# Starting the second layer inside the first layer's last batch, and folding the experts' biases in beside the fifth unit

## The chip, the cores and the metric

The kernel runs on one core of a Trainium2 chip. A core has five engines with an instruction queue each: TensorE (PE, matrix products), VectorE (DVE), ScalarE (ACT), GpSimd (POOL) and SyncE (SP), which here issues most DMA transfers. An engine works through its own queue in order and waits on semaphores for the others. The metric is the device time of one execution in microseconds (us), as a median over several runs.

## The reference

Two layers on an image stack x of shape 4 batches x 32 x 128 x 128, with a residual around each.

```python
# layer 0, Fourier neural operator with attention over the 32 images of a batch
xn = inorm(xa)
k, q, v = fno_layer(xn, K...), fno_layer(xn, Q...), fno_layer(xn, V...)   # 32 heads
p_attn = softmax(einsum('bntk,bnsk->bnts', qf, kf) / sqrt(Hs * Ws))
p = fno_layer(einsum('bnts,bnsk->bntk', p_attn, vf), P...)
a = inorm(p + xa)
m = fno_layer(inorm(a), m0..., inner_norm=True, act=True)    # gelu
m = fno_layer(m, m1..., inner_norm=True)
x = x + inorm(m) + a

# layer 1, on 4 x 4096 tokens of 128 channels; attention in 16 pieces of 1024 tokens
f, g = x @ W1[:h], x @ W1[h:]
scores = einsum('bija,a->bij', tanh(f[:, :, None] + g[:, None] + b1), w2[:, 0]) + b2
e = exp(scores) * strictly_lower_triangle
t = t + (e / (e.sum(-1) + 1e-10)) @ layernorm(t)
# experts: softmax router, best 2 of 8, renormalised
t = t + sum of the two experts' (layernorm(t) @ expert_w + expert_b) by their weights
```

The excerpt is shortened: in the attention of layer 1 the scores are made from the normalised tokens too, and layer 0's own input is group normalised.

## The kernel before, in words

**Layer 0** is the function `layer0`, ordered by a tile scheduler from its data flow and program order. It goes through four batches `b`. For each there are: spectra of 32 images (matrix products with Fourier matrices); `attention_weights`, whose scores come from a loop over 17 columns of modes (L473 to L479: a product `pa` or `pb` on DVE or POOL, then four products on PE into `sp`) and end in `sc`, its maximum `mx` (L509) and the softmax; the value products, which multiply rows of spectra `xb`, fetched by SP in many loads (L702), with the constants `gb` (L717, L719) and contract them (`po`, L722); `py` (L739), the inverse transforms `four` (L257) with `q` added up (L752); a first set of spectra; Gelu (L847); a second set of spectra (`forward`: `pz` L233, `px` L242 and L243, weights L797 to L804); the last inverse transforms, whose updates (L905) give x1, stored in DRAM by SP (L910) in four stores per batch. `attention_weights` of the next batch is called inside the batch before; that of batch 0 is called ahead of the loop, after the constants `mcw`, `energy` and `cross` of the two multiplier layers (L591 to L613), which wait for `mcw_raw` to be loaded.

Pools of SBUF memory in layer 0: constants (with the large `gb`), images (two slots), groups, small, modes, a large one, and `xb` (four buffers). Two PSUM banks have the tag "wide", of which short products use one at a time.

**Layer 1** is `layer1`, called when layer 0 has returned and its pools are closed. It has 16 chunks `c` of 8 blocks of 128 tokens. To prepare a chunk is: load `xc` from x1 (SP), norm (`bn_stats`, `bn_aggr`, a power on POOL, and the scaling that gives `kx`), transposes `pt` (L1065) and their copy `xt` (L1066), products `pz` with `mk` and `mq` (L1082, L1093), an Exp on ACT each (L1083, L1094), a scaling on POOL (L1085), and copies between partitions by DMA (`kf`, `ke`, `qf`; `prepare` has them). The tanh is a rational function of these exponentials: for three groups of hidden units, PE forms a denominator `d` and a numerator `n` (L1297).

A unit is a stretch of 512 queries against a few blocks of keys. The loop over units `u` stands under a manual schedule, so it runs as it is written: `products(u)` (the `d` of unit u beside the `n` of unit u-1), Ln of `d` (L1350), n times r (L1355, DVE), two additions on POOL (L1358, L1359), Exp(-Ln) (L1362), Exp of the score (L1366), and the mask and attention product `po` of units further back (L1316). Preparation of the next chunks (`todo`) and output of finished ones (`ended`) are lists of small pieces, each with a cost on DVE and POOL and a kind that says whether it uses the spare PSUM bank "m"; after every unit some are taken from them by these costs and by the unit at which they are due.

Ahead of the loop stood the opening (L928 to L1100): identity, row of parameters, router `wr` and experts `we`, `eb` loaded; biases folded into the weights by three products `pm` with a matrix `mean` (L972 to L984), all through bank "m"; `mq` and `mk` (L997), constants `sgv`, `off`, `kmul`; chunk 0 prepared whole, chunk 1 loaded and normed (on DVE, POOL's power apart); then unit 0.

Of the kernel before, what the change touches and what calls it, by code (L numbers as in the profile page):

```python
# [7 lines left out]
F32 = mybir.dt.float32  # L8
AF = mybir.ActivationFunctionType
ALU = mybir.AluOpType  # L10
AX = mybir.AxisListType
PSUM = bass.MemoryType.PSUM

P = 128
B, T, H, C = 4, 32, 128, 128
# [5 lines left out]
A = 16  # L21
GROUP_SIZES = (6, 5, 5)
DSCALE = 128.0
NE = 8
IC = 1024
NB = IC // P
# [5 lines left out]
B1, W2, RB = 11, 27, 43  # L32
NSMALL = 51
# [41 lines left out]
NM = KX * KY  # L75
# [29 lines left out]
def layer0(  # L105
    tc, x, kq_modes, kq_mirror, vcw, pcw, m0cw, m1cw, mcol0, heads, heads_row, small_row, by_p, inv_cols, dram, x1
# [4 lines left out]
    const, ps, images = (p.__enter__() for p in pools)  # L111
# [21 lines left out]
    def columns(n):  # L133
# [25 lines left out]
    gb = const.tile([P, 2, 2, NM], F32, name="gb")  # L159
# [7 lines left out]
        tc.tile_pool(name="l0_modes", bufs=1),  # L167
    ]
    grp, small, modes = (p.__enter__() for p in work)
# [409 lines left out]


# [44 lines left out]
    prep_pool.__exit__(None, None, None)  # L625
    work = [tc.tile_pool(name="l0_big", bufs=1), tc.tile_pool(name="l0_xb", bufs=4)]
    big, late = (p.__enter__() for p in work)
    pools += work
    weights = attention_weights(0, front)

    for b in range(B):
# [63 lines left out]
        for x0 in range(0, KX, NK):  # L695
# [36 lines left out]
            nc.scalar.copy(rs[:, x0 : x0 + nk].rearrange("p x y -> p (x y)"), po)  # L732
        yf = big.tile([P, T, 2, KY], F32, name=f"yf_{b}", tag="spec")
# [126 lines left out]
        if b + 1 < B:  # L860
            normed = image_sums(b + 1, loaded)

# [53 lines left out]
def layer1(tc, x1, w1t_in, signs, vec17, expert_w, expert_b, router_w, small_row, out):  # L916
    nc = tc.nc
    nblk = T
    pools = [
        tc.tile_pool(name="l1_const", bufs=1),  # L920
        tc.tile_pool(name="l1_keys", bufs=2),
        tc.tile_pool(name="l1_work", bufs=2),
        tc.tile_pool(name="l1_small", bufs=2),
        tc.tile_pool(name="l1_ps", bufs=1, space=PSUM),
    ]
    const, keys, work, small, ps = (p.__enter__() for p in pools)

    tc.keep_in_program_order(nc.scalar.preload_act_table_set("natural_log_exp_and_others"))  # L928
    ident = const.tile([P, P], F32, name="ident1")
    make_identity(nc, ident)  # L930
    par = const.tile([P, NSMALL], F32, name="par1")
    nc.sync.dma_start(out=par, in_=small_row.partition_broadcast(P))
    nhalf = const.tile([P, 1], F32, name="nhalf1")
    nc.vector.memset(nhalf, -0.5)
    wr = const.tile([P, NE], F32, name="wr")
    nc.sync.dma_start(out=wr, in_=router_w)
    we = const.tile([P, NE, C], F32, name="we")
    nc.scalar.dma_start(out=we, in_=expert_w.rearrange("e d c -> d e c"))

    later = const.tile([P, 2, P], F32, name="later")  # L940
    nc.gpsimd.memset(later, 1.0)
    nc.gpsimd.affine_select(
        out=later,
        in_=later,
        compare_op=ALU.is_gt,
        fill=0.0,
        base=0,
        pattern=[[0, 2], [1, P]],
        channel_multiplier=-1,
    )  # L950

    rank = const.tile([P, NE], F32, name="rank")
    for e in range(NE):
        nc.vector.memset(rank[:, e : e + 1], float(NE - e))

    centre = const.tile([P, P + 1], F32, name="centre")
    nc.vector.tensor_scalar(centre[:, :P], ident, 1.0 / C, None, ALU.subtract)
    nc.vector.memset(centre[:, P:], 1.0 / C)

    banks = ["m"]  # L960

    def misc(name):
        banks.append(banks.pop(0))
        return ps.tile([P, 512], F32, name=name, tag=banks[-1])

    mean = const.tile([P, P], F32, name="mean")
    nc.vector.memset(mean, 1.0 / C)
    eb = work.tile([P, NE, C], F32, name="eb", tag="xt", bufs=1)  # L970
    nc.scalar.dma_start(
        out=eb.rearrange("p e c -> p (e c)"),  # L972
        in_=expert_b.rearrange("e c -> (e c)").partition_broadcast(P),
    )
    for w, row in (
        (wr, par[:, RB : RB + NE]),
        (we[:, :4].rearrange("p e c -> p (e c)"), eb[:, :4].rearrange("p e c -> p (e c)")),
        (we[:, 4:].rearrange("p e c -> p (e c)"), eb[:, 4:].rearrange("p e c -> p (e c)")),
    ):
        n = w.shape[1]  # L980
        pm = misc("pm")[:, :n]
        nc.tensor.matmul(pm, mean, w, start=True, stop=True)
        nc.vector.tensor_tensor(w, w, pm, ALU.subtract)
        nc.vector.scalar_tensor_tensor(w, row, 1.0 / C, w, ALU.mult, ALU.add)  # L984

    sg = const.tile([A + 1, P], F32, name="sg")
    nc.sync.dma_start(out=sg, in_=signs)
    w1t = const.tile([A, 2, P], F32, name="w1t")  # L990
    nc.sync.dma_start(out=w1t, in_=w1t_in)
    v17 = const.tile([A + 1, 2], F32, name="v17")
    nc.sync.dma_start(out=v17, in_=vec17)
    mq, mk = (const.tile([P, P], F32, name=n) for n in ("mq", "mk"))
# [6 lines left out]
    sgv = const.tile([P, 2], F32, name="sgv")  # L1001
    nc.vector.tensor_copy(sgv, pv[:, :2])

    one = const.tile([P, 1], F32, name="one1")
# [4 lines left out]
    off = const.tile([P, 2], F32, name="off")  # L1009
# [3 lines left out]
    kmul = const.tile([P, 1], F32, name="kmul")  # L1013
# [10 lines left out]
    def norm_pieces(src, dst, nb, beside=True):  # L1024


        st = small.tile([P, NB, 6], F32, name="st", tag="ln_st", bufs=3)
        mv = small.tile([P, NB, 2], F32, name="mv", tag="ln_mv", bufs=3)
        r = small.tile([P, NB], F32, name="r", tag="ln_r", bufs=3)
        mr = small.tile([P, NB], F32, name="mr", tag="ln_mr", bufs=3)  # L1030
        engine = nc.gpsimd if beside else nc.vector

        def stats(k0):
            for k in range(k0, k0 + 2):
                nc.vector.bn_stats(st[:, k], src[:, k])

        def aggregate(k0):
            for k in range(k0, k0 + 4):
                nc.vector.bn_aggr(mv[:, k], st[:, k])

        def scale():
            v = slice(0, nb)
            engine.tensor_scalar(r[:, v], mv[:, v, 1], 1e-5, None, ALU.add)
            nc.gpsimd.tensor_tensor(r[:, v], r[:, v], nhalf.to_broadcast([P, nb]), ALU.pow)
            engine.tensor_tensor(mr[:, v], mv[:, v, 0], r[:, v], ALU.mult)
            engine.tensor_scalar(mr[:, v], mr[:, v], 1.0, None, ALU.subtract)

        def apply(k0):
            for k in range(k0, k0 + 2):
                engine.tensor_scalar(  # L1050
                    dst[:, k], src[:, k], r[:, k : k + 1], mr[:, k : k + 1], ALU.mult, ALU.subtract
                )

        sums = [(NONE, 0.6, 0.0, lambda k=k: stats(k)) for k in range(0, nb, 2)]
        after = [(NONE, 0.6, 0.0, lambda k=k: aggregate(k)) for k in range(0, nb, 4)]
        after += [gap, (NONE, 0.0, 2.3, scale), gap]
        for k in range(0, nb, 2):
            after += [(NONE, 0.0, 1.6, lambda k=k: apply(k)), gap]
        return sums, after
# [8 lines left out]
    def prepare(b, i0, own, beside):  # L1068
# [4 lines left out]
        xc = work.tile([P, NB, C], F32, name="xc", tag="xc", bufs=4)  # L1073
        nc.sync.dma_start(out=xc, in_=x1[b, i0 : i0 + NB].rearrange("t w c -> w t c"))
        own_kx = kx[:, i0 : i0 + NB]
        xt = work.tile([P, IC], F32, name="xt", tag="xt", bufs=1)
        qe, qf = (work.tile([P, IC], F32, name=n, tag=n, bufs=3) for n in ("qe", "qf"))

        def as_keys(h):
# [4 lines left out]
            ks = work.tile([P, 512], F32, name="ks", tag="ks", bufs=1)  # L1084
# [13 lines left out]
        load = [(NONE, 0.0, 0.0, lambda: None), gap] * 2  # L1098
        sums, after = norm_pieces(xc, own_kx, NB, beside)
# [4 lines left out]
        return (qe, qf), load + sums + after, pieces  # L1104
# [114 lines left out]
    chunks = [(b, i0) for b in range(B) for i0 in range(0, nblk, NB)]  # L1219
# [10 lines left out]
    state = {}  # L1230
    sums = {}
    live = {}

    def begin(c, beside=True):
        b, i0 = chunks[c]
        if i0 == 0:

            own = (keys.tile([P, nblk, C], F32, name=f"kx_{b}", tag="kx"),) + tuple(
                keys.tile([P, nblk * P], F32, name=f"{n}_{b}", tag=n) for n in ("ke", "kf")
            )  # L1240
        else:
            own = state[c - 1][0]
        qs, norm, pieces = prepare(b, i0, own, beside)
        state[c] = (own, qs)
        return norm, pieces

# [87 lines left out]
    ]  # L1334
    norm, pieces = begin(0, beside=False)
    norm_1, todo = begin(1, beside=False)
    for piece in norm + pieces + norm_1:
        piece[-1]()
# [4 lines left out]
    with tc.manual_schedule():  # L1343
        for u in range(len(units) + 4):
# [35 lines left out]

            if starts and u >= starts[0][0] and not todo:
                _, c, end = starts.pop(0)
                todo = sum(begin(c), [])
# [34 lines left out]
    for p in reversed(pools):  # L1418
        p.__exit__(None, None, None)
# [72 lines left out]
```

## Time and profile before

| | us |
|---|---|
| median of 3 runs | 3216.72 (3215.26 to 3219.33) |
| the profiled execution, its time | 3214.14 |
| its span | 3212.4 |
| PE busy | 2971.1 (92%) |
| ACT busy | 2323.7 (72%) |
| DVE busy | 2317.7 (72%) |
| POOL busy | 2134.2 (66%) |
| last matmul of layer 0 (L257) starts at | 1092.64, for 1.14 |
| first score product of unit 0 (`d`, L1297) | 1126.64 |
| Ln of unit 1 (L1350) | 1139.11 |

Times in the trace are counted from the span's start. A line of a timeline or of the chain of waits starts with its start and its duration; for a timeline, brackets at its end give how long the engine was idle before, and what it was waiting for. `x8` is the number of instructions joined in the line. The busy shares are means over both layers: layer 0 takes about the first third of the span.

### The profile page before, as it was taken

How to read it: one execution, taken by the hardware profiler on the slowest of the kernel's cores; microseconds unless marked ns; L12 is line 12 of the kernel's file. 1: busy time of each engine (PE TensorE's matmuls, PEld its weight loads, DVE VectorE, ACT ScalarE, POOL GpSimd, SP SyncE). 2: the span in 40 equal slices, each digit the busy share in tenths (PEclk: the TensorE clock that was granted, in tenths of full speed). 3: DMA queues.
4: the chain of work that ended last, by engine and by line, in shares of the span. 5: the costliest groups of instructions: out<-in, count | busy, mean ns of one | idle time of the engine just before them, and what ended most of it. 6: DMA issues, size and time to landing. Idle time of an engine off the chain costs nothing.

```text
span 3212.4 us, 53393 instructions
## 1 busy us (share of the span) xinstructions
PE 2971.1 (92%) x19698; PEld 1558.3 (49%) x19698; DVE 2317.7 (72%) x5072; ACT 2323.7 (72%) x3205; POOL 2134.2 (66%) x1879
## 2 busy tenths in 40 slices
PE   7899899899898699999999999999999999999997
PEld 5378367458558544444344443444444434444443
DVE  5767767768777556777666868866777777687887
ACT  2344344354344389999999999998999999999992
POOL 1631641461460278878788897889878889888773
PEclk7899899999998799999999999999999999999998
DMA  6301310230130111010110000011100010101000
GB/s 137 102 25 24 100 50 3 63 108 1 39 107 1 55 45 30 7 31 8 30 37 24 14 24 14 8 32 30 29 24 14 14 37 24 37 1 31 14 14 14
DMA packets 151925, 112.57 MB, mean 35 GB/s; under 512 B 36750, under 2 KB 140273, under 8 KB 151057
## 3 DMA queue, kind: packets, MB, share of 16 engines
q1 hardware_dynamic: 135825, 103.40, 12.0%
q10 hardware_dynamic: 15840, 5.77, 0.8%
q8 instruction: 156, 2.56, 0.3%
q14 instruction: 104, 0.85, 0.1%
HBM read 68.16 MB, written 20.00 MB: 27 GB/s over the span
## 4 chain that ended last, share of the span: by engine, by line
PE 59%; POOL 11%; ACT 8%; DVE 7%; issue 5%; DMA 0%; POOLq 0%; DVEq 0%; ACTq 0%; SPq 0%
PE d L1297 19%; PE po L1316 11%; PE px L1185 6%; ACT r L1350 4%; PE n L1297 4%; PE po L722 3%; POOL e L1359 3%; POOL e L1358 3%; PE four L257 2%; PE pv L252 2%; PE px L243 2%; PE px L242 2%; POOL kx L1050 1%; ACT e L1366 1%; PE pz L233 1%
## 5 line engine op out<-in xcount | busy, mean ns | idle before, releaser
L1355 DVE TENSOR_TENSOR r<-n,r 128x1024 f32<-128x1024 f32 (+1 forms) x1056 | 962.1, 953 | 479.9 <-PE n L1297 392.5
L1358 POOL TENSOR_TENSOR e<-r 128x512 f32<-128x512 f32 x528 | 673.0, 1275 | 268.7 <-DVE r L1355 268.1
L1350 ACT ACTIVATE r<-d 128x1024 f32<-128x1024 f32 (+1 forms) x1056 | 792.9, 802 | 65.5 <-PE n L1297 58.8
L1362 ACT ACTIVATE r<-r 128x1536 f32<-128x1536 f32 x528 | 783.5, 1484 | 16.7
L1359 POOL TENSOR_TENSOR e<-e,r 128x512 f32<-128x512 f32 x528 | 671.2, 1271 | 41.4
L1297 PE MATMUL d<-qe,ke 32*128 32x512 f32 (+3 forms) x2304 | 610.0, 604 | 38.3 <-ACT r L1350 36.5
L1316 PE MATMUL po<-e,kx 128*128 128x512 f32 (+3 forms) x1152 | 594.7, 605 | 15.0 <-POOL e L1371 15.0
L1297 PE MATMUL n<-qe,ke 32*128 32x512 f32 (+3 forms) x2304 | 607.4, 603 | 0.0
L1297 PE MATMUL d<-qf,kf 32*128 32x512 f32 (+3 forms) x2304 | 554.8, 556 | 0.0
L1297 PE MATMUL n<-qf,kf 32*128 32x512 f32 (+3 forms) x2304 | 554.5, 556 | 0.0
L1189 DVE SCALAR_TENSOR_TENSOR xc<-px,wgt,xc 128x128 f32<-128x128 f32 x1024 | 358.3, 350 | 41.2 <-PE px L1185 10.4
L1366 ACT ACTIVATE e<-e 128x512 f32<-128x512 f32 x528 | 325.6, 617 | 65.1 <-POOL e L1359 64.3
L1316 PEld LDWEIGHTS po<-e,kx 128*128 128x128 f32 x1152 | 175.6, 188 | 393.5 <-issue 310.1
L1297 PEld LDWEIGHTS d<-qe,ke 32*128 32x128 f32 x2304 | 177.4, 184 | 359.7 <-ACT r L1350 340.3
L717 POOL TENSOR_TENSOR u<-xb,gb 128x858 f32<-128x858 f32 (+1 forms) x120 | 234.8, 1987 | 115.1 <-PE po L722 104.7
L1297 PEld LDWEIGHTS d<-qf,kf 32*128 32x128 f32 x2304 | 221.5, 187 | 177.1 <-issue 164.7
L804 POOL TENSOR_TENSOR spec<-spec,part 128x264 f32<-128x264 f32 x64 | 55.0, 860 | 377.2 <-DVE part L801 173.6
L1185 PE MATMUL px<-we,x2t 128*128 128x512 f32 x512 | 265.2, 603 | 6.9 <-DVE xc L1189 6.0
L719 DVE TENSOR_TENSOR u<-xw,gb 128x858 f32<-128x858 f32 (+1 forms) x200 | 206.5, 1083 | 48.5 <-PE po L722 32.4
L1297 PEld LDWEIGHTS n<-qf,kf 32*128 32x128 f32 x2304 | 228.9, 186 | 19.8 <-issue 12.5
L722 PE MATMUL po<-u,pr 128*32 128x429 f32 (+1 forms) x1280 | 187.7, 537 | 18.3 <-POOL u L717 8.7
L1297 PEld LDWEIGHTS n<-qe,ke 32*128 32x128 f32 x2304 | 177.8, 183 | 10.0 <-DVE r L1355 1.2
(353 smaller groups left out, 4185.9 us busy)
## 6 DMA issues: line engine op xcount, KB each, us to landing
xb<-xd SPq DMA_DIRECT2D x128, 214.5 KB
xc<-x SPq DMA_DIRECT2D x31, 512.0 KB
x<-x SPq DMA_DIRECT2D x16, 512.0 KB
qf<-qe SPq DMA_DIRECT2D x64, 128.0 KB
out<-xc SPq DMA_DIRECT2D x15, 512.0 KB
xb<-xd SPq DMA_DIRECT2D x32, 198.0 KB
gb<-gd SPq DMA_DIRECT2D x4, 1056.0 KB
x<-in_x SPq DMA_DIRECT2D x8, 512.0 KB
```

What stands on the lines that cost most here:

```text
L717: nc.gpsimd.tensor_tensor(u, xb, gk, ALU.mult)
L722: nc.tensor.matmul(po[32 * j : 32 * j + 32], pr[:, i, k], u[:, r], start=i == 0 and k == 0, stop=i == 3 and k == 1,)
L1185: nc.tensor.matmul(px, x2t[:, k * P : (k + 1) * P], we[:, e0 : e0 + 4], start=True, stop=True)
L1189: nc.vector.scalar_tensor_tensor(xc[:, k], px[:, e], wgt[:, k, e0 + e : e0 + e + 1], xc[:, k], ALU.mult, ALU.add)
L1297: nc.tensor.matmul(o, k, q, start=turn == 0 or g > 0, stop=turn == 1 or g > 0)
L1316: nc.tensor.matmul(sums[c, h][:, q0 : q0 + c1 - c0], kx[:, jb], e[:, c0:c1], start=jb == 0, stop=is_last and q0 > 2 * P, skip_group_check= ...
L1350: nc.scalar.activation(r[:, g], d, AF.Ln, scale=1.0 / DSCALE)
L1355: nc.vector.tensor_tensor(r[:, g], part, r[:, g], ALU.mult)
L1358: nc.gpsimd.tensor_tensor(e, r[:, 1], r[:, 2], ALU.add)
L1359: nc.gpsimd.tensor_tensor(e, e, r[:, 0], ALU.add)
L1362: nc.scalar.activation(r, r, AF.Exp, scale=-1.0)
L1366: nc.scalar.activation(e, e, AF.Exp)
```

## The change

`layer1` becomes a generator with two parts. `kernel` starts it, hands its `send` to `layer0` as `first`, and lets it run on when layer 0 has ended. Layer 0 calls `first` in batch 3, after the last Gelu's table switch, in the place where the other batches do the sums of the next one's images.

- The first part makes what chunk 0 needs (`ident`, `nhalf`, three small loads, `mq`, `mk`, `sgv`, `off`, `kmul`), loads chunks 0 and 1 into `spare`, a free image slot, by two loads of 512 KB on SP, norms both, and does chunk 0's transposes, products, Exps, scalings and copies. It uses layer 0's PSUM tiles "wide", and SBUF in a new pool on the right side, which takes the place of `gb`, `modes` and `xb`: these now lie on that side and are given up in batch 3 after the value products. The scheduler puts its instructions where their operands are ready.
- The second part makes the other constants and begins with the units. Chunks whose number divides by 3 take their `qe`, `qf` from that pool, others from the work pool with two buffers in place of three.
- The three products that fold in the biases, with their DVE work, become `biases()`, called once in unit 4, ahead of that unit's pieces. `eb` shares its memory with `x2` in place of `xt`.
- In layer 0, `attention_weights(0, front)` and the pools it needs stand ahead of `mcw`, `energy`, `cross`, no longer behind them.

Order on the engines: all orders are as before but for batch 0's attention (DVE), batch 3 of layer 0, and layer 1 up to unit 5. Steady units are untouched, and the number of instructions is the same on each engine.

```diff
@@ layer0
-    const, ps, images = (p.__enter__() for p in pools)
+    right = [tc.tile_pool(name="l0_gb", bufs=1, side="right"), tc.tile_pool(name="l0_modes", bufs=1, side="right")]
+    const, ps, images, values, modes = (p.__enter__() for p in pools + right)
...
+    prep_pool.__exit__(None, None, None)
+    pools.append(tc.tile_pool(name="l0_big", bufs=1))
+    right.append(tc.tile_pool(name="l0_xb", bufs=4, side="right"))
+    big, late = (p.__enter__() for p in (pools[-1], right[-1]))
+    weights = attention_weights(0, front)
     mcw, energy, cross = [], [], []
...
-    weights = attention_weights(0, front)
...
             nc.scalar.copy(rs[:, x0 : x0 + nk].rearrange("p x y -> p (x y)"), po)
+        if b + 1 == B:
+            for p in reversed(right):
+                p.__exit__(None, None, None)
...
         if b + 1 < B:
             normed = image_sums(b + 1, loaded)
+        else:
+            first((ps, images))
@@ layer1
+    before, images = yield
+    first_pool = tc.tile_pool(name="l1_first", bufs=1, side="right")
+    first = first_pool.__enter__()
+    spare = images.tile([P, T, C], F32, name="spare", tag="x")
...
+    def misc(name):
+        if not pools:
+            return before.tile([P, 512], F32, name=name, tag="wide")
...
+    FIRST = (slice(0, NB), slice(0, NB)), (slice(3 * NB, 4 * NB), slice(NB, 2 * NB))
...
+    _, pieces = begin(0)
+    kx = state[0][0][0]
+    norms = [normed(spare[:, r], kx[:, i], 0, i.start, False) for r, i in FIRST]
+    for piece in norms[0] + pieces + norms[1]:
+        piece[-1]()
+    yield
...
-    for w, row in (
-        (wr, par[:, RB : RB + NE]),
...
+    def biases():
+        for w, row in (
+            (wr, par[:, RB : RB + NE]),
+            (we[:, :4].rearrange("p e c -> p (e c)"), eb[:, :4].rearrange("p e c -> p (e c)")),
+            (we[:, 4:].rearrange("p e c -> p (e c)"), eb[:, 4:].rearrange("p e c -> p (e c)")),
+        ):
+            n = w.shape[1]
+            pm = misc("pm")[:, :n]
+            nc.tensor.matmul(pm, mean, w, start=True, stop=True)
+            nc.vector.tensor_tensor(w, w, pm, ALU.subtract)
+            nc.vector.scalar_tensor_tensor(w, row, 1.0 / C, w, ALU.mult, ALU.add)
...
-    norm, pieces = begin(0, beside=False)
-    norm_1, todo = begin(1, beside=False)
-    for piece in norm + pieces + norm_1:
-        piece[-1]()
+    _, todo = begin(1)
...
+            if u == 4:
+                biases()
             if starts and u >= starts[0][0] and not todo:
@@ kernel
+        second = layer1(tc, x1, *weights, out)
+        next(second)
         layer0(
...
             x1,
+            second.send,
         )
-        layer1(
...
+        for _ in second:
+            pass
```

## The prediction

> **What bounds the kernel now.** I read the page first, for what is busy on the whole and where it isn't.
>
> ```profile
> PE 2971.1 (92%) x19698; PEld 1558.3 (49%) x19698; DVE 2317.7 (72%) x5072; ACT 2323.7 (72%) x3205; POOL 2134.2 (66%) x1879
> ...
> PEclk7899899999998799999999999999999999999998
> ```
>
> TensorE (PE) bounds the mean, but a mean says nothing of one place. The clock row dips near slices 14 and 15, where layer 0 ends. So next the chain of waits there: start, length, what it followed.
>
> ```profile
> 1093.81 0.35 SPq L932
> ...
> 1094.21 5.26 DMA wr<-in_router_w
> ...
> 1103.35 2.09 PE pm L982 x2
> ...
> 1114.27 2.04 DVE kx L1050 x8
> ...
> 1126.64 2.00 PE d L1297 x2
> ...
> 1130.65 3.71 PE d L1297 x6
> ```
>
> Layer 0's last matmul ends at 1093.8. Then one thing after another: a load of the router (5.26 us), biases of the experts, mq and mk, chunk 0's norm, its transposes, its products `pz`. Layer 1's first score product `d` starts at 1126.6. For 33 us no engine is the bound; latencies are. The windows (time, then busy of PE, its weight loads, DVE, ACT, POOL, then PE's clock, DMA share, GB/s) show this stretch and the first units:
>
> ```profile
> 1094.00:1095.00 1.00, 0.00 (x0) 0.00 (x0) 1.00 (x12) 0.00 (x0) 0.90 (x4) 0.62 1.02 278
> ...
> 1127.00:1139.00 12.00, 12.00 (x39) 5.17 (x39) 0.69 (x1) 4.16 (x5) 1.56 (x1) 0.52 0.29 66
> 1139.00:1142.00 3.00, 2.34 (x35) 2.10 (x36) 2.42 (x3) 2.86 (x3) 1.58 (x2) 1.00 0.00 0
> 1142.00:1152.00 10.00, 9.30 (x62) 4.08 (x58) 5.47 (x6) 9.83 (x14) 9.10 (x9) 1.00 0.22 51
> ```
>
> From 1139 on ACT is the bound (9.83 of 10). So whatever brings ACT's units forward shortens the whole run, and what delays ACT there lengthens it. I measure the boundary by the start of the second unit's Ln (L1350), at 1139.11 in the timeline of ACT.
>
> **The change, part by part** (negative: shorter).
>
> *A. Batch 0's attention goes ahead of the mode constants.* DVE's timeline:
>
> ```profile
> 82.23 0.29 DVE L591 COPY mcw<-mcw_raw 128x66 f32<-128x66 f32 x1 [2.54 <-DMA mcw_raw<-in_m1cw]
> 82.44 1.21 DVE L473 TENSOR_TENSOR pb<-xp,xm 128x1024 f32<-128x1024 f32 x1
> ...
> 85.10 1.21 DVE L473 TENSOR_TENSOR pa<-xp,xm 128x1024 f32<-128x1024 f32 x1
> ...
> 107.33 0.68 DVE L509 TENSOR_REDUCE mx<-sc 64x16 f32<-64x512 f32 x1 [5.28 <-PE sc L498]
> ```
>
> Products `pa`, `pb` on DVE feed PE at 1.13 us apiece. Before, DVE waits 2.54 us for `mcw_raw`, and small constants stretch the run: 0.21, then 2.66−1.13=1.53 between the rows at 82.44 and 85.10, then 0.38 and 0.64 in the next two distances: 2.76. Afterwards all constants stand behind the last `pa`, where DVE waits 5.28 us for `sc` anyway, which hides their 2.8 us. That is −5.3 at best. If POOL's `pb` (1.88 us each, two per three steps: 3.8 against DVE's four at 4.5) or the images' loads gate instead, it is 0. The next row is DVE's own pitch, so I take −5.2. Without the 5.28 us wait it would keep 2.5.
>
> *B. Batch 3 carries two loads and chunk 0's and 1's norms.* Two 512 KB loads into `spare` go on SP's queue at batch 3's start. They wait for the stores of x1 of batch 2 to finish; the `xb` loads of the value products stand behind them. SP's last such store is issued near 892.2, the next `xb` at 895.4, and of four `xb` buffers three are ahead, each good for some 3.4 us of value products, 10 us: taken as 0. On DVE: 16 bn_stats of 0.21, 16 aggregates of 0.07, 16 scalings of 0.26 and a few small ones, 9 us; and two POOL powers of 1.67, on a POOL that is idle for 31.67 us up to 989.38. DVE's timeline has the cover:
>
> ```profile
> 963.28 1.12 DVE L180 TENSOR_SCALAR yf<-py 128x512 f32<-128x512 f32 x1 [6.98 <-PE py L739]
> 967.30 0.28 DVE L180 TENSOR_SCALAR yf<-py 128x64 f32<-128x64 f32 x1 [2.90 <-PE py L739]
> 971.21 0.69 DVE L752 TENSOR_TENSOR q<-q,four 128x512 f32<-128x512 f32 x1 [3.63 <-PE four L257]
> ```
>
> 6.98+2.90+3.63 is 13.5 us of idle time for 9 us. The second power comes late for the first `q` add (about 0.9), and six scalings (1.5) fall into the q stage, where PE is busy 17.30 of 18 us and DVE 13.53; DVE's spare takes about 1.2 of it. So +1.2, from 0.5 to 2.5; with no cover it would be 9.
>
> *C. Chunk 0's keys and queries stand in front of layer 0's last spectra.* PE's idle of 4.63 us before 1031.59 hides the two `pm`. From there PE runs without a gap to 1044 (12.00 of 12 us), so what is added counts in full. At full clock: `pv` and `pc` 0.5; eight transposes 1.1 (four took 0.66 at 1138.86); four `pz` of 0.86, 3.45 (one took 1.13 with its end). Their Exps (0.67 each) stand behind ACT's last Gelus and this row of its timeline:
>
> ```profile
> 1043.21 1.28 ACT L121 ACT_TABLE_LOAD   x1
> ```
>
> Two banks hold `pz`, so the third waits for the first Exp, which may come only after 1044.5. `px` of the next group then follows; by my count it goes from 1046.45 to about 1051.7: +5.3, between 4 (ACT in time) and 12 (PE held until all four Exps are done). POOL's two scalings (1.6 each) lie in an idle POOL, the ten copies of `kf`, `ke`, `qf` on an idle SP, and 44 us ahead of their use.
>
> *D. The boundary.* The first `d` waits for the banks that the last L905 update frees, at 1094.94; nothing else is late (ACT's Ln stands behind the issue of the expert loads, 0.4 us each, done by 1095.5). `d` of unit 0 costs 2.00+3.71=5.7 by the chain's two rows, and from its end (1134.36) to the second Ln passed 4.75. Both ran at half clock. At that price the Ln comes at 1095.0+5.7+4.75=1105.4: −33.7. At full clock both halve, nearly (2.85 and 2.6): 1100.4, −38.7.
> Which clock? The row 1094 to 1095 shows 0.62 already, and 1095 to 1100 has 0.50; the matmuls before it are the same in both kernels. Getting it back took all 12 us of gapless PE from 1127 to 1139. The Trainium skill ("TensorE: Matmul & The Clock Gate", Part 1, "What you observe") says that the transition "happens around 4µs into sustained matmul activity". By it the clock would be whole at 1099, `d` done at 1099.9 and the Ln at 1102.5: −36.6. The trace disagrees with it here (12 us), so I take the row: −33.7. Both ends, −31.5 (the third unit cold as well) and −38.7, go into the range.
>
> *E. Biases in unit 4.* One bank serves three products. By PE's timeline unit 5's `d` starts at 1151.46. Now `pm` of the router waits for its subtraction, behind `r<-n` that ends at 1151.47; then twice 0.96 for `pm` at full clock and 0.69 for DVE's subtraction; then `pz`, 1.06. `d` starts at about 1156.0. ACT's Ln has a little slack, and moves less:
>
> ```profile
> 1150.25 1.50 ACT L1350 ACTIVATE r<-d 128x1024 f32<-128x1024 f32 x2
> ...
> 1154.26 1.50 ACT L1350 ACTIVATE r<-d 128x1024 f32<-128x1024 f32 x2
> ```
>
> from 1154.26 to about 1157.9: +3.65, between 2.5 and 4.5. ACT is full there, so it isn't won back. The loads of the experts are issued at 1095 and used 15 us later; they took under 6.3.
>
> Sum: −5.2+1.2+5.3−33.7+3.65 = −28.75. The profiled execution took 3214.14 us (span 3212.4), so 3185.4; on the median of 3216.72, 2.6 above it, 3188.
>
> **Rivals.**
> 1. *PE stalls behind ACT in layer 0's last batch* (C at 12). For: PE takes its work in order, and Gelus and a table load stand before the Exps. Against: the first `pz` come early in a 12 us stretch in which ACT works 7.18 us. −22: 3195.
> 2. *The early move gives nothing* (A at 0). For: POOL's 3.8 is close to DVE's 4.5. Against: POOL waits for DVE's `pa` there. −23.5: 3193.
> 3. *The boundary closes only by half*, so that the change doesn't do what it says: unit 0 waits for something of layer 0's end that the router's load hid, such as the last stores of x1 (issued at 1095.66). Against: the keys come from a tile of its own, and reads of x1 aren't needed. With 17 us lost of the 34: 3205.
> 4. *Slower:* the loads into `spare` hold SP's queue at batch 3's start. The stores they wait for would have to land late: the first 10 us are covered by `xb` buffers, and the net gain of 29 more, so that it is slower only from a hold of 39 us on; at 45, +6: 3223. Against: a store of 512 KB near 892 needs no such time, as loads at the boundary moved 278 GB/s (the row 1094 to 1095), by which 512 KB take 2 us.
>
> **How the numbers follow.** The likeliest, 0.62: 3188, with its own range 3180 to 3193 (down: D at full clock −5, and B, C, E at their low ends −0.7−1.3−1.15; up: D with a cold third unit +2.2, B and E high +2.1). Rival 1 0.15, rival 2 0.12, rival 3 0.08, rival 4 0.03. Range: 3177 (those low ends, and 3 for the spread of the runs around their median) to 3200 (rivals 1 and 2 together), leaving out rivals 3 and 4 and some tails. A difference under 0.2%, 6.4 us, can't be told from none. Faster 0.96, within 0.02, slower 0.02.
>
> **What would show each step.** A: no wait for `mcw_raw` inside the `pa` run, and `mx<-sc` near 102. B: first `q` add about 1 us later against the end of `py`; SP's first `xb` of batch 3 not later. C: gap between the last Gelu and `px` of the second group 5 us longer. D: `d` of unit 0 right behind the last L905, clock 0.50 under it, second Ln 10 us later. E: an idle ACT of 3 to 4 us ahead of unit 5's Ln. The prediction is wrong if the first `d` waits longer than 2 us for anything, if `xb` loads starve, or if PE shows gaps over 5 us between the Gelus and `px`.

## The result, and the profile after

The changed kernel took 3193.26 us (median of 4 runs, 3183.4 to 3196.28) beside 3215.99 for the kernel before: a ratio of 0.9923, with a 95% interval of 0.9900 to 0.9947. Measured again, beside the experiments below, it took 3195.28 beside 3219.55: 0.9917, 0.9903 to 0.9931. So it is faster by 23 to 24 us, where 28.75 were forecast; the forecast range held the time (3177 to 3200), while the likeliest case's own range (3180 to 3193) ends just below it. The profiled execution of the changed kernel took 3196.28 us, its span is 3194.2.

Lines of kernel.py have moved: `four` is L261, the last updates L914, `d` and `n` L1349, Ln L1399, `pm` L1172. These are the page's busy shares and the clock row of the changed kernel:

```profile
PE 2961.2 (93%) x19698; PEld 1556.6 (49%) x19698; DVE 2318.6 (73%) x5072; ACT 2324.8 (73%) x3205; POOL 2135.8 (67%) x1879
...
PEclk8899999899998799999999999999999999999998
```

Sums hardly move; the work is the same. The chain of waits at the boundary, changed kernel:

```profile
1098.27 5.13 PE four L261 x24
...
1103.42 1.14 DVE x L914 x4
1104.56 0.14 issue
1104.69 3.79 PE d L1349 x8
```

The first `d` starts 0.14 us after the last update. All of the router's load, folds, norms, transposes and `pz` are gone from this place. ScalarE's timeline shows the Ln that I measured by (second row), and what came later:

```profile
1108.48 1.51 ACT L1399 ACTIVATE r<-d 128x1024 f32<-128x1024 f32 x2 [8.28 <-PE d L1349]
1113.53 1.51 ACT L1399 ACTIVATE r<-d 128x1024 f32<-128x1024 f32 x2 [2.02 <-PE n L1349]
...
1124.67 1.50 ACT L1399 ACTIVATE r<-d 128x1024 f32<-128x1024 f32 x2
1135.77 1.51 ACT L1399 ACTIVATE r<-d 128x1024 f32<-128x1024 f32 x2 [2.28 <-PE n L1349]
```

Two things strike at once. Layer 0 ends at 1104.55, no longer at 1094.94, so something in it cost much more than the +1.3 of steps A to C. And between the Ln of units 4 and 5 lie 11.1 us.

To find where it went I cut each profiled execution into stretches between the same instructions. Each number is a distance in a timeline, in us: `pa`, `mx` and Ln count by their starts, the others by their ends; "changed" gives the first and the second profile of the changed kernel, "before" the profile of the prediction and a second one, `before_again`.

| stretch | before | changed | forecast of the difference |
|---|---|---|---|
| first `pa` to `mx` of batch 0 | 36.2, 44.7 | 36.3, 36.8 | −5.2 (A) |
| last `py` of batch 3 to the last Gelu | 75.9, 73.2 | 75.2, 78.3 | +1.2 (B) |
| last Gelu to last `px` | 19.05, 19.04 | 25.82, 25.81 | +5.3 (C) |
| last `px` to the last scalars `cq` | 13.69, 13.69 | 18.45, 16.79 | 0 |
| `cq` to the last update of layer 0 | 19.0, 19.1 | 20.3, 18.9 | 0 |
| last update to Ln of unit 1 | 44.2, 44.7 | 8.98, 8.98 | −33.7 (D) |
| Ln of unit 4 to Ln of unit 5 | 4.01, 4.01 | 11.10, 8.22 | +3.65 (E) |

Those stretches repeat well. Two others don't, in any kernel: the first `pa` starts near 61 or near 70 (before: 71.1 and 60.9), and from `mx` of batch 0 to the first `py` of batch 3 it takes between 851 and 862 us. So a comparison of just two profiles is off by up to 10 us before batch 0 is done, and the ends of two spans say less than the table. From the Ln of unit 20 to the end of the span every profile takes 2002.4 to 2005.9 us, the three with the old layer 1 as well as the others: two buffers in place of three for `qe` and `qf` cost nothing that shows.

### The profile page after: what moved, and what is told of

Read it like the earlier page. It is cut to its first block, busy times and chain, and to the rows that moved or that the text cites. A ratio compares the mean times of both kernels' runs of the same rounds, so it can differ in the third digit from the quotient of the medians.

```text
span 3194.2 us, 53401 instructions
## 1 busy us (share of the span) xinstructions
PE 2961.2 (93%) x19698; PEld 1556.6 (49%) x19698; DVE 2318.6 (73%) x5072; ACT 2324.8 (73%) x3205; POOL 2135.8 (67%) x1879
## 4 chain that ended last, share of the span: by engine, by line
PE 56%; POOL 12%; ACT 9%; DVE 7%; issue 6%; DMA 0%; POOLq 0%; DVEq 0%; ACTq 0%; SPq 0%
PE d L1349 18%; PE po L1368 10%; PE px L1255 6%; ACT r L1399 4%; PE n L1349 3%; POOL e L1408 3%; POOL e L1407 3%; PE po L726 3%; PE four L261 2%; PE pv L256 2%; PE px L247 2%; PE px L246 2%; ACT e L1415 2%; POOL kx L1014 2%; DVE r L1404 2%
## 5 line engine op out<-in xcount | busy, mean ns | idle before, releaser
L1399 ACT ACTIVATE r<-d 128x1024 f32<-128x1024 f32 (+1 forms) x1056 | 793.4, 803 | 71.5 <-PE n L1349 57.8
L1349 PE MATMUL d<-qe,ke 32*128 32x512 f32 (+3 forms) x2304 | 606.7, 603 | 39.7 <-ACT r L1399 36.4
L1349 PE MATMUL n<-qe,ke 32*128 32x512 f32 (+3 forms) x2304 | 606.2, 601 | 0.0
L1349 PE MATMUL n<-qf,kf 32*128 32x512 f32 (+3 forms) x2304 | 552.3, 554 | 0.0
L1349 PE MATMUL d<-qf,kf 32*128 32x512 f32 (+3 forms) x2304 | 550.8, 554 | 0.0
L1349 PEld LDWEIGHTS d<-qe,ke 32*128 32x128 f32 x2304 | 176.9, 184 | 359.5 <-ACT r L1399 340.1
L1349 PEld LDWEIGHTS d<-qf,kf 32*128 32x128 f32 x2304 | 220.5, 186 | 176.9 <-issue 164.2
L1349 PEld LDWEIGHTS n<-qf,kf 32*128 32x128 f32 x2304 | 228.0, 185 | 18.6 <-issue 11.2
L1349 PEld LDWEIGHTS n<-qe,ke 32*128 32x128 f32 x2304 | 177.8, 183 | 9.3 <-DVE r L1404 0.9
```

Of the source, the lines that this page charges most:

```text
L1349: nc.tensor.matmul(o, k, q, start=turn == 0 or g > 0, stop=turn == 1 or g > 0)
L1399: nc.scalar.activation(r[:, g], d, AF.Ln, scale=1.0 / DSCALE)
```

## The experiments

Each but before_again, which ran once, was timed in the same rounds as runs of the kernel before; each was profiled. Ratios are to the kernel before.

**after_again** is the changed kernel, unedited.

> The changed kernel as it is, as the measure for the runs beside it. The first measurement gave 3193.3 against 3216.0, 22.7 less. If the shortfall against the forecast (28.75 less) is of the kernel and not of that one chip, the gain is 20 to 25 again; if it was an accident of the clock's phase, it comes out at 27 to 31.

Measured: 0.9917 (0.9903 to 0.9931), 24 us less. The shortfall against 28.75 repeats: it is of the kernel.

**before_again** is the kernel before, profiled once more.

> The kernel before, profiled a second time, to see which of its stages repeat. If the first stage's length is a matter of the clock's phase and not of the change, the first pa comes near 61 or near 71 here as it does in the changed kernel. If the clock's fall between the last px of layer 0 and cq is the change's doing, that stretch takes 13.7 us again, as in the first profile; if it is chance, 16 to 19 as in the changed kernels.

Measured: 3216.44 us. The first `pa` came at 60.9, so the early start isn't the change's doing. The stretch after the last `px` was 13.69 again; so the longer one is. The early start also showed that DVE's wait for `mcw_raw` ends at nearly the same time, at 81.25 here and 82.23 in the first profile. DVE's timeline of this run:

```profile
81.25 0.20 DVE L591 COPY mcw<-mcw_raw 128x66 f32<-128x66 f32 x1 [11.82 <-DMA mcw_raw<-in_m1cw]
```

It waited 11.82 us, not 2.54: the earlier `pa` starts, the longer the wait that step A takes away.

**a_undone** and **a_only**: step A taken out of the changed kernel, and put alone into the kernel before.

```diff
 # a_undone, against the changed kernel
-    weights = attention_weights(0, front)
     mcw, energy, cross = [], [], []
...
     nc.vector.tensor_mul(pv, pv, psw2)
+    weights = attention_weights(0, front)
```

> The changed kernel with batch 0's attention weights back behind the mode constants, nothing else moved. The prediction's step A expects it 5.2 us slower than the changed kernel. What the trace after suggests (ScalarE copies xw from xb before spt, waits until the loads of xb land at 89.7, and TensorE's clock halves while it waits for spt, so that the gain in the pa run is lost before mx) expects no difference: within 2 us.

> The kernel before with step A alone: batch 0's attention weights ahead of the mode constants. The prediction's step A expects 5.2 us less than the kernel before, and mx 5 to 8 us earlier for the same start of pa (from the first pa to mx 36 in place of 44.7 with an early start, 31 in place of 36.2 with a late one). If later stages take it back, because their half clocks fall differently, mx is earlier and the time within 2 us of the kernel before.

Measured: a_undone 3200.58 (0.9928, 0.9911 to 0.9946), 5 us above after_again by the medians, with overlapping intervals. a_only 3212.48 beside 3221.30: 0.9972 (0.9961 to 0.9982), 9 us less, 6 to 13 by the interval. From `pa` to `mx` a_undone took 44.5 us with its early start, as before_again. a_only took 30.8 with a late one, where the kernel before took 36.2: 5.4 less. So step A is real and was worth at least what was forecast. My suspicion that it gives nothing came from setting one early start beside one late start, and it fell. What had fed it is there, though. ScalarE's timeline of the changed kernel (early start):

```profile
89.73 0.52 ACT L715 COPY xw<-xb 128x429 f32<-128x429 f32 x1 [28.87 <-DMA xb<-xd]
90.68 0.52 ACT L715 COPY xw<-xb 128x429 f32<-128x429 f32 x1 [0.42 <-DMA xb<-xd]
91.13 0.58 ACT L491 COPY spt<-sp 128x512 f32<-128x512 f32 x1
```

`spt` stands behind two copies that wait for `xb`. TensorE waits 3.53 us for it, its clock halves, and from the end of the `pa` products to `mx` it takes 9.2 us in place of 3.7. With an early start step A thus gives 8 us (44.7 to 36.8) and not some 14, as DVE's wait of 11.82 and the constants' 2.8 would make together. That the wait for `xb` is what takes the rest is read from the trace; no run took it away.

**spt_dve** lets VectorE copy `spt` in batch 0; it was expected to be idle there.

```diff
-        nc.scalar.copy(spt, sp)
+        (nc.scalar.copy if b else nc.vector.tensor_copy)(spt, sp)
```

> The changed kernel, and in batch 0 alone spt is copied by VectorE, which is idle there, in place of ScalarE, where it stands behind two copies that wait for loads of xb. If the wait on ScalarE's queue is what swallowed step A, mx starts 3 to 6 us earlier (2.9 us of waiting, and up to 2.9 more if TensorE's clock stays whole in the three products sc) and the kernel is faster by 2 to 6 us. If the value products behind it wait for xb or for the clock anyway, mx is earlier and the time unchanged.

Measured: 3195.02 (0.9921, 0.9904 to 0.9937), no difference to after_again. It tells nothing of that wait: the run started late, where `xb` is there in time, and VectorE's copy came behind the mode constants, 2.0 us after the last `sp` had ended. From that end to `mx` it took 7.3, where ScalarE's copy takes 3.7 in the other late starts; so the edit made `mx` later and not earlier.

**fold_late** spreads the folds over units 8, 9 and 10.

```diff
-    def biases():
+    def biases(which):
         for w, row in (
...
-        ):
+        )[which : which + 1]:
...
-            if u == 4:
-                biases()
+            if 8 <= u <= 10:
+                biases(u - 8)
```

> The changed kernel with the three folds one by one in units 8, 9 and 10, where no product pz needs the bank m, in place of all three in unit 4. In the trace after, unit 5's Ln comes 7.1 us later than a unit takes; the prediction had 3.65. If the three round trips through one bank in front of pz are the cost, nearly all of it comes back: 5 to 7 us faster than the changed kernel. If it is the work itself (three products and six VectorE instructions in a stretch where ScalarE is full), at most 2 us come back.

Measured: 3192.17 (0.9906, 0.9888 to 0.9923), 3 us below after_again by the medians. The trace says it more sharply: unit 5's Ln comes 4.01 us after unit 4's, as before the change, and from there to the Ln of unit 20 the units take 1.0 us longer than in the changed kernel. So the folds cost 1.0 us there, in place of 7.1 or 4.2. ScalarE's timeline of fold_late, units 4 and 5, then two at a fold, 3.84 us apart where the units beside them take 3.44:

```profile
1126.19 1.50 ACT L1399 ACTIVATE r<-d 128x1024 f32<-128x1024 f32 x2
1130.21 1.50 ACT L1399 ACTIVATE r<-d 128x1024 f32<-128x1024 f32 x2
...
1148.03 1.51 ACT L1399 ACTIVATE r<-d 128x1024 f32<-128x1024 f32 x2
1151.87 1.51 ACT L1399 ACTIVATE r<-d 128x1024 f32<-128x1024 f32 x2 [0.29 <-PE n L1349]
```

**gap_fill** adds four products that keep TensorE at work in a gap of 3.2 us.

```diff
         spec, sq = spectra(1, gl)
+        for k in range(4 if b + 1 == B else 0):
+            warm = ps.tile([P, 264], F32, name="warm", tag="wide")
+            nc.tensor.matmul(
+                warm, rows, sq[:, 0, T - 8 :].rearrange("p t k -> p (t k)"), start=True, stop=True
+            )
```

> The changed kernel with four products of 264 columns, whose result nobody reads, right behind the last px of layer 0's batch 3, in the 3.2 us in which TensorE waits for the spectra. In five profiles of changed kernels the clock halved 4.2 us after that px, and the stretch from it to cq took 16.8 to 18.5 us, 13.7 before. If TensorE's idle time in that gap makes the clock fall, the stretch comes back to 13.7 to 14.5 and the kernel is 3 to 5 us faster; if the fall has another cause, it stays above 16.5.

Measured: 3181.25 beside 3216.92: 0.9885 (0.9867 to 0.9904). That is some 10 us under after_again by the ratios, where 3 to 5 were expected; the intervals just touch. The stretch from the last `px` to `cq` took 13.63, which is 3.1 to 4.8 of it. Windows of the changed kernel first (after the times: PE busy, its weight loads, DVE, ACT, POOL, the clock), then of gap_fill:

```profile
1066.59:1070.00 3.41, 1.04 (x10) 1.07 (x11) 2.70 (x5) 0.00 (x0) 1.68 (x1) 1.00 0.00 0
1070.00:1080.24 10.24, 10.24 (x51) 10.24 (x49) 5.57 (x18) 2.13 (x5) 0.00 (x0) 0.50 0.01 2
```

```profile
1070.00:1073.51 3.51, 2.82 (x18) 2.24 (x17) 2.81 (x6) 0.00 (x1) 1.68 (x1) 1.00 0.00 0
1073.51:1083.75 10.24, 7.67 (x68) 7.15 (x66) 7.69 (x29) 3.97 (x11) 0.00 (x0) 1.00 0.01 2
```

From the first `pv` behind the gap to the last, TensorE works 13.52 us without a break in the changed kernel, 10.24 of them at half clock, and 8.80 in gap_fill. The clock falls here only with TensorE's idle time in that gap: shown, since work without any use in it prevents the fall, in all three runs that have it. The idle time alone isn't enough, as the kernel before has it, too.

Why it fell after the change and not before, when the gap is 3.20 us in both, isn't settled. The recorded clock is 0.50 or 1.00, for whole multiples of 3.41 us. Counted from the end of the half clock ahead of it, the gap leaves TensorE 1.04 us of work in one such step after the change (30%), and 1.51 us before it (44%), in the kernel before's window:

```profile
1063.53:1066.95 3.42, 1.51 (x15) 1.54 (x15) 2.71 (x4) 0.41 (x1) 1.59 (x1) 1.00 0.00 0
```

Step C's added 6.8 us moved the gap against these steps, which would explain it if a share of work between the two decided. One run speaks against so simple a rule. In `fill`, below, the same step of 3.41 us held 1.68 us of work, more than in the kernel before, and the clock fell right behind it, 1.73 us after the last `px`:

```profile
1065.80:1069.21 3.41, 1.68 (x16) 1.51 (x14) 2.15 (x5) 0.56 (x2) 1.27 (x2) 1.00 0.00 0
1069.21:1072.62 3.41, 1.94 (x9) 1.97 (x10) 2.71 (x4) 0.00 (x0) 1.15 (x1) 0.50 0.00 0
```

What decides beside the gap stays open.

**keys_late** calls chunk 0's pieces after batch 3's last scalars.

```diff
             weights = attention_weights(b + 1, front)
+        else:
+            first(None)
...
-    for piece in norms[0] + pieces + norms[1]:
+    for piece in norms[0] + norms[1]:
+        piece[-1]()
+    yield
+    for piece in pieces:
         piece[-1]()
     yield
```

> The changed kernel with chunk 0's transposes, products and Exps called after batch 3's last scalars, so that they are meant for TensorE's idle 8.6 us there, no longer in front of the last spectra. If step C's price is the place in front of the spectra, the stretch from the last Gelu to the last px goes from 25.8 back to about 19, and with it the next one from 17 to 18 back to 13.7: together 8 to 11 us, less 1 to 4 that the Exps now take from ScalarE ahead of the last scalings. If the same work simply delays the next stage, nothing is won: within 2 us.

Measured: 3189.93 (0.9910, 0.9894 to 0.9927), some 2 us under after_again by the ratios, where 4 to 10 were expected. Last Gelu to last `px` took 21.68: 4.1 of the 6.8 us went. The 2.6 us left may lie in what stayed in place (`pv`, `pc`) and in the clock, half for 13.7 us around it, for 10.2 before; they weren't taken apart. The next stretch stayed long (18.33), for two reasons. The clock fell all the same. And the scheduler didn't put the transposes and `pz` into the 8.6 us of idle time: they ran from 1069.60 to 1075.49, ahead of the last `pv`, inside this stretch, and left a wait of 6.49 us. So it isn't the run that it was meant to be.

**fill** adds nine idle products, meant for the 8.6 us ahead of the last transforms.

```diff
             inverse(spec[:, i], last)
+            for k in range(9 if b + 1 == B and g == 8 else 0):
+                warm = ps.tile([P, 264], F32, name="warm", tag="wide")
+                nc.tensor.matmul(warm, rows, spec[:, :4].rearrange("p t k -> p (t k)"), start=True, stop=True)
```

> The changed kernel with nine products of 264 columns, whose result nobody reads, in TensorE's 8.6 us of waiting ahead of the last inverse transforms. If the half clock at the boundary comes from that wait, the clock is whole from the last transforms into the first units: d of unit 0 to the second Ln takes 5.5 to 7 us in place of 8.8, and the transforms themselves shorten by up to 1.5; 2 to 5 us in all. If the transforms don't load TensorE enough to keep the clock, it has fallen again by the first d, and there is no difference.

Measured: 3193.47 (0.9920, 0.9904 to 0.9935), no difference. Its windows:

```profile
1089.70:1103.40 13.70, 12.00 (x54) 11.71 (x55) 7.25 (x25) 9.16 (x23) 7.46 (x4) 0.50 0.40 116
1103.40:1106.80 3.40, 1.88 (x16) 1.51 (x16) 2.57 (x19) 0.98 (x1) 0.72 (x2) 0.99 0.04 5
1106.80:1113.60 6.80, 6.80 (x34) 3.96 (x32) 0.69 (x1) 2.99 (x3) 0.00 (x0) 0.50 0.72 233
```

The scheduler set the idle products ahead of the last 16 `pv` (from 1080.62, for 4.17 us), so they shortened the wait from 8.59 to 4.77 us and didn't fill it. The clock fell in it, came back after 13.7 us, and fell once more under the first `d`.

**gap_fold** and **gap_fold_keys** put gap_fill and fold_late together, and keys_late as well.

> The changed kernel with the four idle products of gap_fill and the folds in units 8 to 10 of fold_late. If both causes are as those runs showed, they add up: 4.8 us (no fall of the clock in the last stage) and 3 to 6 us (no stall in unit 5) against the changed kernel, so 8 to 11 less, some 3184 beside a kernel before of 3217. If they overlap, it is no better than gap_fill alone.

> gap_fold with chunk 0's transposes, products and Exps called late, too, as in keys_late. There the stretch from the last Gelu to the last px fell by 4.1 us (25.8 to 21.7), and the last stage grew by 1. With the clock kept whole by the idle products I expect 3 us less than gap_fold; if the late place delays the last inverse transforms once the clock is whole, no difference or a loss of up to 3.

Measured: gap_fold 3187.19 beside 3221.30 (0.9891, 0.9877 to 0.9904), which can't be told from gap_fill alone, though its trace has both repairs (13.64 and 4.02). gap_fold_keys 3178.15 (0.9861, 0.9846 to 0.9876): 43 us under the kernel before, and by its interval better than the changed kernel, too. It is 9 us under gap_fold, where 3 were expected. The stretches give 5.0 of them: 4.1 less to the last `px`; 1.5 and 1.3 more in the next two, with chunk 0's products inside the first of them (15.17 in place of 13.64 at whole clock); and 3.6 less at the boundary. In it the clock was whole in the first units:

```profile
1078.50:1092.20 13.70, 9.47 (x44) 9.47 (x45) 7.26 (x25) 10.76 (x28) 9.42 (x4) 0.50 0.40 107
1092.20:1096.00 3.80, 2.51 (x22) 2.28 (x20) 2.19 (x15) 2.01 (x3) 0.73 (x2) 1.00 0.49 139
1096.00:1101.36 5.36, 4.75 (x38) 3.02 (x39) 1.16 (x10) 3.00 (x4) 0.00 (x0) 1.00 0.78 245
```

From the first `d` to unit 1's Ln it took 5.24 us, where 8.84 passed in the changed kernel: the price of the cold clock at the boundary is 3.6 us, by this one profile.

## Why the prediction was right, and by how much not

The direction, the main term (D) and the range were right. The number came nearer than its terms: A and D gave 3.0 us more than forecast, which hid a third of what the others cost. And the time is what rival 2 was given (3193), though rival 2 didn't happen: the sum alone can't tell the two apart. Term by term, from the stretches:

- **A**, −5.2 forecast: −5.4 with a late start (36.2 to 30.8 in four kernels that have step A), −8 with an early one. The pitch of DVE's rows was the right neighbour to cost it by; that the wait depends on the start was unknown. Rival 2 is out. How much of it the later batches keep isn't settled: `mx` to `py` varies by 11 us, from batch 0 to batch 3.
- **B**, +1.2: some +1.7 (76.8 on the mean of ten changed kernels, 75.1 of three without the change to batch 3), within the scatter. Rival 4, the slower one, is out: the longest wait of a load into `spare` for the stores of x1 was 2.8 us in the waits of SP's queue, where 39 would have been needed.
- **C**, +5.3: +6.8. The mechanism is the one forecast, within its bounds. The sum assumed full clock. TensorE's timeline of the changed kernel:

```profile
1033.08 0.58 PE L960 MATMUL pv<-v,sg 17*128 17x2 f32 x2
...
1037.60 1.87 PE L1029 MATMUL pt<-ident,kx 128*128 128x128 f32 x8
...
1040.66 1.13 PE L1064 MATMUL pz<-spare,mk 128*128 128x512 f32 x2
```

The clock was half until 1039.29: `pv`, `pc` and the transposes, forecast at 1.6, moved what follows by 3.1; the `pz`, behind it, ran at full. The prediction could have seen it, as the window of the kernel before, which it read for TensorE's 12.00 of 12, shows a clock of 0.68:

```profile
1032.00:1044.00 12.00, 12.00 (x77) 12.00 (x77) 7.82 (x29) 7.18 (x16) 0.00 (x0) 0.68 0.01 2
```

  Rival 1, at 12, is out: ScalarE reached the first Exp at 1041.88, and TensorE never waited for it.
- **Next stretch**, 0 forecast: +3.1 to +4.8. This is the term that was missing, put at nothing without a look at the clock. I asked what C's work delays, and not what its length does to the clock in a gap behind it. The last stretch added 0.8 on the mean of five.
- **D**, −33.7: −35.2 against the first profile. Rival 3 is out, as the first `d` waited for nothing after the last update. The cold clock was right. By the rule of the Trainium skill ("TensorE: Matmul & The Clock Gate", Part 1, "What you observe") I estimate that it would have been whole some 4 us after the start; it was whole only at 1114.4, 10 us after, and TensorE had had work almost without a break since 1091. The first `d` took 3.79 in place of the 5.7 that I had added up, and from its end to the second Ln passed 5.05 in place of 4.75:

```profile
1104.69 2.08 PE L1349 MATMUL d<-qe,ke 32*128 32x512 f32 x4 [1.31 <-DVE x L914]
1106.54 1.95 PE L1349 MATMUL d<-qf,kf 32*128 32x512 f32 x4
```

  Here the eight products of `d` run two at a time. In the kernel before, with a `pz` between its halves, the first two and the last two ran one after the other, so that the row's price didn't carry over. At full clock 5.24 were measured for the 5.45 forecast.
- **E**, +3.65: 7.0 to 7.1 in four profiles, 4.2 in the three others that have the folds in unit 4 (after_again, fill, gap_fill). The forecast counted the three round trips at full clock, and where the clock stayed whole, in those three, its bounds held (2.5 to 4.5). In the four the clock fell between the products. VectorE's timeline of the changed kernel and TensorE's:

```profile
1125.99 1.28 DVE L1174 SCALAR_TENSOR_TENSOR wr<-par,wr 128x8 f32<-128x8 f32 x1
1127.19 0.67 DVE L1173 TENSOR_TENSOR we<-we,pm 128x512 f32<-128x512 f32 x1
1127.90 1.25 DVE L1174 SCALAR_TENSOR_TENSOR we<-eb,we 128x512 f32<-128x512 f32 x1
```

```profile
1126.01 1.12 PE L1172 MATMUL pm<-we,mean 128*128 128x512 f32 x2 [0.80 <-DVE wr L1173]
1127.92 1.99 PE L1172 MATMUL pm<-we,mean 128*128 128x512 f32 x2 [0.78 <-DVE we L1173]
1130.69 2.07 PE L1064 MATMUL pz<-xt,mk 128*128 128x512 f32 x2 [0.78 <-DVE we L1173]
```

The clock was half from 1128.04 to 1134.87, so the second `pm` and `pz` took 2 us instead of the 1.13 of after_again. That is 1.8 of the 2.9 us between 7.1 and 4.2; the rest falls on the first products of unit 5 behind them, until the clock was whole again. The same gaps of 0.8 us between the products stand in the three profiles in which it stayed whole, so they alone don't explain the fall.

And in all of them the update of 8 columns took 1.25 to 1.28, where the same instruction took 0.17 in the kernel before. POOL's timeline of the changed kernel, and VectorE's of the kernel before:

```profile
1125.97 1.28 POOL L1407 TENSOR_TENSOR e<-r 128x512 f32<-128x512 f32 x1
```

```profile
1100.47 0.17 DVE L984 SCALAR_TENSOR_TENSOR wr<-par,wr 128x8 f32<-128x8 f32 x1
```

The update ends at 1127.27, just when POOL's addition `e<-r` ends (1127.25). The Trainium skill ("SBUF — State Buffer", "Who interferes with whom") says that a VectorE instruction with two SBUF inputs contends with a GpSimd instruction that reads SBUF, and that issue order decides who blocks. The trace agrees, and with POOL idle, before, there was nothing to block. I had taken durations from rows with an idle POOL.

Sum of what was measured: A −6.7 (between its two values), B +1.7, C +6.8, next +4.1 and E +5.9 (means of seven profiles), last +0.8, D −35.2: −22.6, beside −22.7 and −24.3 of the two measurements. That it meets them so closely is partly chance, as the stretch from `mx` to `py`, which is left out, varies by 11 us. So the forecast of 28.75 was too large mainly by the clock: in the stretch behind C, where gap_fill shows it, and in C and in E, where it is read from the traces.

## What to carry to other kernels

Work that is moved into a busy stage costs more than its own time where it shifts a gap of TensorE or leaves new ones: ask of every gap of about 3 us or more, downstream too, whether the clock survives it. Idle products can fill such a gap (four in 3.2 us did), if the scheduler puts them into it (nine for 8.6 us went ahead of it). Set stretches between equal instructions side by side, in several profiles of both kernels, before explaining the difference of two spans. Small chores with round trips through one bank belong in units that don't need that bank, one chore per unit (1.0 us in place of 4.2 or 7.1).

## What the runs showed of the hardware that I had not expected

- The clock can stay at half through long work of TensorE: in the changed kernel from 1087.1 to 1114.4, 27.3 us, though from 1091 on TensorE had a matmul running nearly all the time (windows below). So it was in three of the ten profiles of changed kernels (the first, a_undone and spt_dve). In the seven others, with the same `four` and `pv`, it was whole after 13.7 us; in six of these it fell again 3.41 us later, close to the first `d`, and only in gap_fold_keys it stayed. The share of work doesn't tell them apart: TensorE had worked 2.69 of the 3.41 us (1090.74 to 1094.16) when it fell again in gap_fold, and 2.59 (1092.12 to 1095.53) when it stayed in gap_fold_keys. What makes the one or the other wasn't found.

```profile
1087.06:1104.55 17.49, 12.31 (x56) 12.02 (x56) 9.43 (x40) 11.96 (x28) 10.13 (x6) 0.50 0.32 90
1104.55:1113.50 8.95, 8.77 (x37) 4.77 (x38) 1.15 (x13) 2.99 (x3) 0.00 (x0) 0.50 0.57 181
```

- A gap of 3.20 us let the clock fall in one place of the changed kernels (seven profiles without idle products in it), and never in the same gap of the kernel before and a_only (three profiles).
- The start of a run has two lengths, in both kernels: in the kernel before, TensorE ran at half clock for 47.8 us from 29 on in the first profile, for 17.1 us in the second, and its first `pa` came 10 us later in the first.
